# Turning listed expert rows in 32 by 32 blocks on VectorE, with rows and first weights loaded in a matching order

## The chip, the cores and the metric

The kernel runs as one program on one core of a Trainium2 chip. The metric is the device time of one execution in microseconds. Six executions were timed; the figure to compare with is their median. One further execution was recorded by the hardware profiler, and every duration below is from that one.

The core's engines are TensorE (PE; its weight loads are listed as PEld), VectorE (DVE), ScalarE (ACT), GpSimd (POOL) and SyncE (SP). In this kernel SP only issues transfers. POOL does some arithmetic and issues the transfers that go by a list of rows. All transfers run on the core's 16 DMA engines.

## The reference, cut to what matters

Inputs are float32: x is (8, 512, 256), w1 is (8, 256, 1024) and w2 is (8, 1024, 256), one slice for each of eight experts.

```
h = layernorm(x) * (1 + ca) + sa
x = x + ga * linear_attention(h)                 # 16 heads, causal, rope
h = layernorm(x) * (1 + cb) + sb                 # 4096 tokens of 256
probs = softmax(h @ router_w.T)                  # 8 experts
topv, topi = top_k(probs, 2); topv = topv / (sum(topv) + 1e-9)
for each token t and each of its two experts e:
    y[t] += topv[t, e] * (gelu(h[t] @ w1[e]) @ w2[e])
return x + gb * y
```

sa, ca, ga, sb, cb and gb come from a small product of the conditioning input. The kernel computes an expert only for the tokens that chose it, which are 8192 pairs of token and expert.

## The kernel before

**Attention and routing.** The eight sequences are worked one after another, each in four chunks of 128 tokens (the functions early, middle and late). rows_of forms each token's second-layernorm row. route picks its two experts. It gives each pair of token and expert a slot in the DRAM table slots, which has a region per expert. POOL's indirect transfers (L963, eight a sequence) scatter the rows there. A row of slots has 521 numbers: 256 of the token's normed row (D), the token's number (TID), eight weights (CW to GATE) and 256 of the gate row.

**Experts in blocks.** Filled slots are worked in blocks of 128 rows (nt = 1, a single) or 256 rows of one expert (nt = 2, a pair). The list TAKE says how many blocks are taken after each sequence; plan computes on the chip which ones, and plan_rest the rest after the last sequence. In all 40 blocks run: 13 singles and 27 pairs, and the first nine are singles. For each block:

- fetch has SP read the expert's number and load its w1 (L1216, 1 MB, as 128 partitions by 2 by 1024) and w2 (L1221, 1 MB, as 128 by 8 by 256). It reads the first slot and loads the rows into r (L1227). Tiles w1, w2 and r have three buffers each. The rows wait for the scatters of the last sequence; in plan_rest for the zeroing of the table's ends too.
- turn_rows has PE turn each 128x128 piece of the rows against an identity matrix into the PSUM tile x_ps, and ACT copies x_ps to xT (two buffers), so that the 256 numbers of a row lie along partitions. DVE forms the block's weights cw and the token list to.
- PE multiplies xT by w1 into h_ps, ACT applies gelu into g, and PE multiplies g by w2 into y_ps (one buffer). A product of 32-bit numbers is two matmul instructions, so a block has 32 of them for h_ps, and 16 for y_ps for each 128 rows.
- finish has DVE scale y_ps by cw and the gate into y, and POOL adds y to the table acc, or to the output near the end, by an indirect transfer (L1321). Before the last blocks, eight copies take acc to the output.

In partition terms w1's partition p holds rows p and 128 + p of the expert's 256 input rows (k = 0 and 1), and xT's partition p holds features p and 128 + p.

**What sets the order.** The kernel first records all work in a Plan. Each piece has an engine, a cost in us, a level and what it reads and writes. Plan.run then simulates the engines and writes out one fixed order for each. Ready work with the lowest level goes first; expert products have the high level 1000 + X.k, so attention comes before them. The engines run their lists strictly in order. All emitted operations of PE, ACT and DVE carry line L220, so they are told apart by tile. SP's transfers use eight completion semaphores in turn, and in the built order a transfer waits for the one eight places before it.

Of the kernel before, what the change touches and what calls it, by code (L numbers as in the profile page):

```python
# [11 lines left out]
I32 = mybir.dt.int32  # L12
# [7 lines left out]
HEADS = 16  # L20
HD = 16
HALF = HD // 2
PAIR = 2 * HD
GH = P // HD
LN_EPS = 1e-5
# [313 lines left out]
def kernel(  # L339
# [57 lines left out]

    SYNC = mybir.DependencyInfo(mybir.DependencyClass.Sync, mybir.DependencyReason.DATA)
    scattered = []
    gathered = []  # L400
    added = []
    copied = []
# [17 lines left out]
    def late_bank(name):  # L420
        return bank(name, "late", 4)
# [462 lines left out]
    def route(q):  # L884
        b, row = q.b, q.row

        def small(shape, tag, dtype=F32):
            return L.tile(p1, shape, tag, f"{tag}_{b}", 1, dtype)

        l3 = q.logits  # L890
        red = small([P, NC, 1], "red")
        pr = small([P, NC, E], "pr")
        dve(V.tensor_reduce, red, l3, us=0.18, axis=AX.X, op=ALU.max)
        dve(V.tensor_sub, pr, l3, red.to_broadcast([P, NC, E]))
        act(pr, pr, AF.Exp)
        dve(V.tensor_reduce, red, pr, us=0.18, axis=AX.X, op=ALU.add)
        dve(V.reciprocal, red, red)

        dve(
            V.scalar_tensor_tensor, pr, pr, LARGE, red.to_broadcast([P, NC, E]), us=0.24,  # L900
            op0=ALU.mult, op1=ALU.mult,
        )

        gt = small([P, NC, E, E], "gt")
        rank = small([P, NC, E], "rank")
        mine = pr.unsqueeze(3).to_broadcast([P, NC, E, E])
        others = pr.unsqueeze(2).to_broadcast([P, NC, E, E])
        dve(V.tensor_sub, gt, others, mine)
        dve(
            V.tensor_tensor, gt, gt, least.unsqueeze(1).to_broadcast([P, NC, E, E]), op=ALU.is_gt  # L910
        )
        dve(V.tensor_reduce, rank, gt, us=0.42, axis=AX.X, op=ALU.add)
        dve(V.scalar_tensor_tensor, pr, rank, 2.0, pr, op0=ALU.is_lt, op1=ALU.mult)

        is_in = small([P, NC, E], "is_in")
        first = small([P, NC, 2, E], "first")
        dve(V.tensor_single_scalar, is_in, rank, 2.0, op=ALU.is_lt)
        at_ps = early_bank(f"at_ps_{b}")
        with L.group("PE", 1.05):
            product(  # L920
                at_ps[:, : NC * E], earlier, is_in.rearrange("p c e -> p (c e)"),
                start=True, stop=False, skip_group_check=True,
            )
            for c in range(NC):

                product(
                    at_ps[:, (c + 1) * E : (NC + 1) * E].rearrange("p (c e) -> p c e", e=E),
                    ones, is_in[:, c, :].unsqueeze(1).to_broadcast([P, NC - c, E]),
                    start=False, stop=(c == NC - 1), skip_group_check=True,
                )  # L930
        dve(V.tensor_reduce, red, pr, us=0.18, axis=AX.X, op=ALU.add)
        dve(V.tensor_scalar_add, red, red, 1e-9 * LARGE)
        dve(V.reciprocal, red, red)
        dve(V.tensor_mul, row[:, :, CW:GATE].of("cw"), pr, red.to_broadcast([P, NC, E]))
        L.do(
            "POOL", 0.15,
            lambda: G.iota(
                row.now()[:, :, TID:CW].bitcast(I32), pattern=[[P, NC], [0, 1]], base=b * S,
                channel_multiplier=1,
            ),  # L940
            w=[row.of("tid")],
        )
        dve(
            V.tensor_tensor, first, rank.unsqueeze(2).to_broadcast([P, NC, 2, E]),
            which.unsqueeze(1).to_broadcast([P, NC, 2, E]), op=ALU.is_equal,
        )
        begin = small([P, E], "begin")
        at = small([P, NC, E], "at")
        where = small([P, NC, 2], "where")
        slot = L.tile(p2, [P, NC, 2], "slot", f"slot_{b}", 2, I32)  # L950
        dve(V.tensor_add, begin, count, first_slot)
        dve(
            V.tensor_add, at, at_ps[:, : NC * E].rearrange("p (c e) -> p c e", e=E),
            begin.unsqueeze(1).to_broadcast([P, NC, E]),
        )
        dve(V.tensor_mul, first, first, at.unsqueeze(2).to_broadcast([P, NC, 2, E]))
        dve(V.tensor_reduce, where, first, us=0.21, axis=AX.X, op=ALU.add)
        dve(V.tensor_copy, slot, where)
        dve(V.tensor_add, count, count, at_ps[:, NC * E : (NC + 1) * E])
        q.scatters = []  # L960

        def scatter(c, j):
            s = nc.gpsimd.indirect_dma_start(  # L963
                out=slots, out_offset=IndirectOffsetOnAxis(ap=slot.now()[:, c, j : j + 1], axis=0),
                in_=row.now()[:, c, :], in_offset=None,
                bounds_check=NONE - 1, oob_is_err=False,
            )
            apart(s, scattered + cleared, "a slot is of one pair of token and expert")
            apart(s, gathered, "blocks that are read are full by then")
            scattered.append(s)  # L970

        L.level += LEVEL["scatter"]
        for c in range(NC):
            for j in range(2):
                q.scatters.append(
                    L.do(
                        "POOL", 1.29, lambda c=c, j=j: scatter(c, j), r=[slot, row], landing=2.0,
                        mb=0.27,
                    )
                )  # L980
                q.scatters[-1].indirect = True


    def spans(small, n, tag):
# [221 lines left out]
    def fetch(block):  # L1206
# [1 line left out]
        L.level = TOP  # L1208
        w1_sb = L.tile(wpool, [P, KD, H], "w1", f"w1_{n}", 3)
        w2_sb = L.tile(wpool, [P, NH, D], "w2", f"w2_{n}", 3)  # L1210
        r = L.tile(pb, [P, 2, ROW], "r", f"r_{n}", 3)
        reg = {}

        def weights1():
            reg["e"] = nc.sync.value_load(block.expert_i.now(), min_val=0, max_val=E - 1)
            nc.sync.dma_start(  # L1216
                out=w1_sb.now(), in_=w1[ds(reg["e"], 1)].rearrange("o (k p) h -> p (o k) h", p=P)
            )

        def weights2():  # L1220
            nc.sync.dma_start(  # L1221
# [2 lines left out]

        def rows():
            at = nc.sync.value_load(block.slot.now(), min_val=0, max_val=NONE)
            got = nc.sync.dma_start(  # L1227
                out=r.now()[:, :nt, :],
                in_=slots[ds(at, nt * P), :].rearrange("(t p) w -> p t w", p=P),
            )  # L1230
            needed = [g for w in block.seen for g in w.given]
            behind(got, needed, "the rows of a block come before it")
            apart(got, [s for s in scattered if s not in needed], "those are of later blocks")
            gathered.append(got)

        L.do("SP", 0.6, weights1, r=[block.expert_i], w=[w1_sb], landing=2.0, mb=1.0)
        L.do("SP", 0.4, weights2, r=[block.expert_i], w=[w2_sb], landing=2.0, mb=1.0)
        L.do("SP", 0.6, rows, r=[block.slot], w=[r], after=block.seen, landing=2.0, mb=0.26 * nt)
        return block, w1_sb, w2_sb, r

    def turn_rows(fetched):

        block, w1_sb, w2_sb, r = fetched
        n, nt = block.n, block.nt
        L.level = 1000 + X.k - 1.5
        rest = block.held is not None
        x_ps = late_bank(f"x_ps_{n}") if rest else early_bank(f"x_ps_{n}")
        w = nt * P
        xT = L.tile(pb, [P, KD, 2 * P], "xT", f"xT_{n}", 2)
        with L.group("PE", 0.11 * 2 * nt, hold=[xT]):  # L1250
            for k in range(KD):
                for t in range(nt):
                    turn(x_ps[:, k * w + t * P : k * w + (t + 1) * P], r[:, t, ts(k, P)])
        L.level = TOP
        copy(xT[:, :, :w], x_ps[:, : KD * w].rearrange("p (k s) -> p k s", k=KD))
        cw = L.tile(pb, [P, 2, 1], "cw", f"cw_{n}", 3)
        cwe = L.tile(pb, [P, 2, E], "cwe", f"cwe_{n}", 3)
        dve(
            V.tensor_mul, cwe[:, :nt], r[:, :nt, CW:GATE],
            block.is_of.unsqueeze(1).to_broadcast([P, nt, E]),  # L1260
        )
        dve(V.tensor_reduce, cw[:, :nt], cwe[:, :nt], us=0.17, axis=AX.X, op=ALU.add)
        to = L.tile(pb, [P, 2], "to", f"to_{n}", 3, I32)
        dve(V.tensor_copy, to[:, :nt], r[:, :nt, TID].bitcast(I32))
        if rest:

            empty = L.tile(pb, [P, 2], "empty", f"empty_{n}", 3, I32)
# [27 lines left out]
    def finish(block, cw, to, r, y_ps):  # L1295
# [3 lines left out]
        for t in range(nt):  # L1299
            dve(  # L1300
                V.scalar_tensor_tensor, y[:, t, :].of(t), y_ps[:, ts(t, D)], cw[:, t, :],
                r[:, t, GATE:], us=0.48, op0=ALU.mult, op1=ALU.mult,
            )
        if block.at_end and X.copies is None:
            def give(b):
# [94 lines left out]
    for b in range(B):  # L1400
# [20 lines left out]
        route(q)  # L1421
        if TAKE[b][0]:
            L.level = 4 * b + 3 + LEVEL["plan"]
            blocks = plan(b, q.scatters)
            experts(blocks)
    L.level = 4 * B
    blocks, others, more_i = plan_rest(q.scatters)

    def all_of(blocks):
        experts(blocks)  # L1430
# [71 lines left out]
```

## Time and profile before

| | |
|---|---|
| median of six runs | 821.68 us (818.67 to 825.2) |
| profiled execution, whole time | 825.21 us |
| its span, first to last instruction | 823.5 us |
| mean granted TensorE clock | 0.986 |
| PE, DVE, ACT, POOL busy | 96%, 46%, 34%, 39% |
| products h_ps and y_ps on PE | 255.7 and 253.6 us busy |
| turns x_ps on PE | 134, 21.5 us busy |
| bytes moved | 154.27 MB, mean 187 GB/s |
| PE busy from 441 to 799 us | 358.0 of 358.0 us |

How to read it: busy time is the sum of the recorded instruction times on an engine; matmuls overlap, so a PE that is always busy is not PE at its peak. A group line gives the line, engine, operation, written and read tiles, shape and count, then busy us and mean ns of one, then the idle time before them and what ended it. A slice line has 40 digits, one for each fortieth of the span, in tenths busy. The DMA share is a mean over the 16 engines.

The first work on experts stands at 133.6 us and the last block's first h_ps at 799.1 us. Until 424 us blocks stand between pieces of attention and routing; from there PE does experts alone, a pair about every 14 us.

### The profile page before, as it was taken

The page shows a single profiled execution, that of the slowest core. Times are in us where ns is not written, and L with a number is a line of the kernel's source. Part 1 is how long each engine was busy: PE and PEld are TensorE (multiplying, and loading weights), DVE is VectorE, ACT ScalarE, POOL GpSimd, SP SyncE. Part 2 cuts the span into 40 slices and gives each one's busy share as a digit, 9 for nine tenths or more (in the row PEclk, how much of TensorE's full clock was granted, in tenths as well). Part 3 has the DMA queues.
Part 4 walks back from the last instruction along what each step waited for, and adds up shares of the span by engine and source line. Part 5 has one row for each costly group of instructions (what it writes and reads, how often), then busy time and mean ns, then how long its engine had stood idle before and what let it go on. Part 6 is the DMA issues. An engine that isn't in the chain of part 4 may idle for free. (4 is left out here: it accounts for less than half of the span.)

```text
span 823.5 us, 15967 instructions
## 1 busy us (share of the span) xinstructions
PE 790.7 (96%) x5998; PEld 657.0 (80%) x5998; DVE 378.0 (46%) x1290; ACT 284.1 (34%) x617; POOL 320.9 (39%) x477
## 2 busy tenths in 40 slices
PE   6899989999998999999999999999999999999995
PEld 3567657767786788789888888888988889898884
DVE  4588978788886878776363010111111111111000
ACT  2546444446564475542232122222121212222120
POOL 4734374638374464726138331312121232130133
PEclk9899998999999999999999999999999999999998
DMA  7320183965664454647579966766766878579932
GB/s 233 98 60 27 59 240 129 341 149 124 199 174 125 141 163 129 214 146 232 166 230 311 299 203 190 231 174 216 240 216 193 271 211 246 173 229 306 310 67 27
DMA packets 95167, 154.27 MB, mean 187 GB/s; under 512 B 6632, under 2 KB 69736, under 8 KB 94960
## 3 DMA queue, kind: packets, MB, share of 16 engines
q1 hardware_dynamic: 79680, 125.22, 48.7%
q0 software_dynamic: 15408, 28.00, 13.5%
q8 instruction: 49, 0.80, 0.4%
q14 instruction: 30, 0.25, 0.1%
HBM read 120.19 MB, written 37.20 MB: 191 GB/s over the span
## 5 line engine op out<-in xcount | busy, mean ns | idle before, releaser
L220 PE MATMUL h_ps<-xT,w 128*128 128x256 f32 (+1 forms) x1280 | 255.7, 349 | 2.6 <-issue 2.6
L220 PE MATMUL y_ps<-w,g 128*128 128x256 f32 x1072 | 253.6, 380 | 0.0
L220 PEld LDWEIGHTS h_ps<-xT,w 128*128 128x128 f32 x1280 | 215.1, 194 | 26.1 <-issue 3.2
L220 PEld LDWEIGHTS y_ps<-w,g 128*128 128x128 f32 x1072 | 200.2, 190 | 26.1 <-issue 0.6
L220 ACT ACTIVATE g<-h_ps 128x512 f32<-128x512 f32 x134 | 80.0, 597 | 307.3 <-PE h_ps L220 307.1
L1321 POOL DMA_INDIRECT acc<-y,to x57 | 90.3, 1584 | 243.2 <-DVE y L220 198.0
L220 DVE SCALAR_TENSOR_TENSOR y<-y_ps,cw,r 128x256 f32<-128x256 f32 x67 | 29.9, 479 | 155.1 <-PE y_ps L220 155.0
L220 DVE TENSOR_TENSOR sm<-s_ps,causal 128x512 f32<-128x512 f32 x128 | 82.1, 678 | 11.9 <-PE s_ps L220 11.9
L963 POOL DMA_INDIRECT slots<-row,slot x64 | 64.8, 1013 | 36.6 <-issue 13.2
L220 PE MATMUL qk_ps<-wqkv_sb,hT 128*128 128x512 f32 x128 | 65.0, 633 | 1.1 <-ACT hT L220 1.0
L220 POOL TENSOR_TENSOR f<-f,t 128x512 f32<-128x512 f32 x32 | 43.4, 1359 | 52.2 <-DVE t L220 41.1
L220 DVE TENSOR_TENSOR cwe<-r,is_of_rest 128x16 f32<-128x16 f32 (+1 forms) x21 | 3.6, 173 | 130.1 <-DMA r<-slots 122.3
L220 PEld LDWEIGHTS s_ps<-qT,kT 32*128 32x128 f32 x1024 | 32.6, 186 | 10.8 <-issue 7.3
L220 PE MATMUL s_ps<-qT,kT 32*128 32x128 f32 x1024 | 39.5, 284 | 0.9 <-ACT logits L220 0.7
L220 PEld LDWEIGHTS qk_ps<-wqkv_sb,hT 128*128 128x128 f32 x128 | 24.0, 202 | 20.2 <-issue 14.2
L220 PE MATMUL v_ps<-wqkv_sb,hT 128*128 128x256 f32 x128 | 36.2, 408 | 2.1 <-ACT hT L220 2.0
L220 PE MATMUL oT_ps<-sm,vz 128*32 128x128 f32 x1024 | 36.8, 276 | 1.3 <-DVE sm L220 1.2
L1321 POOL DMA_INDIRECT out_dram<-y,to x10 | 15.6, 1559 | 52.9 <-DMA out_dram<-acc 23.3
L220 POOL TENSOR_SCALAR mv_f<-mv_f 128x1 f32<-128x1 f32 x32 | 10.2, 318 | 62.5 <-DVE mv_f L220 56.2
L220 PE MATMUL a_ps<-wo,oT 128*128 128x256 f32 x128 | 33.6, 385 | 0.5 <-DVE sm L220 0.4
L220 ACT COPY xT<-x_ps 128x512 f32<-128x512 f32 (+1 forms) x40 | 20.6, 514 | 34.6 <-PE x_ps L220 34.3
L220 PEld LDWEIGHTS oT_ps<-sm,vz 128*32 128x32 f32 x1024 | 26.9, 109 | 6.7 <-DVE sm L220 3.2
(227 smaller groups left out, 998.4 us busy)
## 6 DMA issues: line engine op xcount, KB each, us to landing
w<-in_w_dram SPq DMA_DIRECT2D x80, 1024.0 KB, 5.8
r<-slots SPq DMA_DIRECT2D x27, 521.0 KB, 6.9
row<-modd SPq DMA_DIRECT2D x8, 512.0 KB, 10.1
acc<-x SPq DMA_DIRECT2D x8, 512.0 KB, 3.7
out_dram<-acc SPq DMA_DIRECT2D x8, 512.0 KB, 10.6
x<-in_x_dram SPq DMA_DIRECT2D x7, 512.0 KB, 7.1
r<-slots SPq DMA_DIRECT2D x13, 260.5 KB, 6.8
mod<-modd SPq DMA_DIRECT2D x8, 384.0 KB, 4.5
```

The costliest lines, as they stand in the source:

```text
L220: return method(now(out), *[now(a) for a in args], **{k: now(a) for k, a in kw.items()})
L963: s = nc.gpsimd.indirect_dma_start(out=slots, out_offset=IndirectOffsetOnAxis(ap=slot.now()[:, c, j : j + 1], axis=0), in_=row.now()[:, c, ...
L1321: s = nc.gpsimd.indirect_dma_start(out=out.rearrange("b s d -> (b s) d") if block.at_end else acc, out_offset=IndirectOffsetOnAxis(ap=to.n ...
```

## The change

- A block's 256 features are no longer turned by PE. The first 256 numbers of each listed row go to a new tile sx by four transfers, one for each quarter q of 64 features. Quarter q lands on the 32 partitions 32q to 32q + 31. The partition is the row's place within a group of 32 rows; along the partition lie the groups (4 nt of them), then k of 2, then 32 features. The other 265 numbers of each row go to a smaller r by a fifth transfer.
- One DVE transpose then turns every 32x32 block of sx within its own 32 partitions straight into xT. Partition 32q + c of xT holds features 64q + c and 64q + 32 + c.
- w1 is loaded to match: partition 32q + c holds input rows 64q + 32k + c for k = 0 and 1. This takes two transfers of 512 KB, one for each k, whose source is 4 by 32 by 1024.
- The bank x_ps, its turns on PE and the copy on ACT are gone. TID, CW and GATE are read from r at an offset less by D.
- The list of scatters that a block's rows wait for now holds those of all sequences so far.

In the order built for each engine, PE has the same products as before without the turns. SP issues eight transfers a block instead of three. On DVE the transpose of a block stands in the place where cwe stood, ahead of the y evictions of one or two blocks before it.

```diff
+Q = 32
...
+    scatters = []
...
-                q.scatters.append(
+                scatters.append(
...
-        r = L.tile(pb, [P, 2, ROW], "r", f"r_{n}", 3)
+        sx = L.tile(pb, [P, 8, KD, Q], "sx", f"sx_{n}", 3)
+        r = L.tile(pb, [P, 2, ROW - D], "r", f"r_{n}", 3)
...
-            nc.sync.dma_start(
-                out=w1_sb.now(), in_=w1[ds(reg["e"], 1)].rearrange("o (k p) h -> p (o k) h", p=P)
-            )
+            parts = w1[ds(reg["e"], 1)].rearrange("o (q k c) h -> k (o q) c h", k=KD, c=Q)
+            for k in range(KD):
+                nc.sync.dma_start(out=w1_sb.now()[:, k, :], in_=parts[k])
...
-            got = nc.sync.dma_start(
-                out=r.now()[:, :nt, :],
-                in_=slots[ds(at, nt * P), :].rearrange("(t p) w -> p t w", p=P),
-            )
+            rows_ = slots[ds(at, nt * P), :]
             needed = [g for w in block.seen for g in w.given]
-            behind(got, needed, "the rows of a block come before it")
-            apart(got, [s for s in scattered if s not in needed], "those are of later blocks")
-            gathered.append(got)
+            parts = [
+                (
+                    sx.now()[q * Q : (q + 1) * Q, : 4 * nt].rearrange("p t k c -> p t (k c)"),
+                    rows_[:, q * KD * Q : (q + 1) * KD * Q].rearrange("(t p) c -> p t c", p=Q),
+                )
+                for q in range(P // Q)
+            ]
+            parts.append((r.now()[:, :nt, :], rows_[:, D:].rearrange("(t p) w -> p t w", p=P)))
+            for out_, in_ in parts:
+                got = nc.sync.dma_start(out=out_, in_=in_)
+                behind(got, needed, "the rows of a block come before it")
+                apart(got, [s for s in scattered if s not in needed], "those are of later blocks")
+                gathered.append(got)
...
-        L.do("SP", 0.6, rows, r=[block.slot], w=[r], after=block.seen, landing=2.0, mb=0.26 * nt)
+        L.do("SP", 1.0, rows, r=[block.slot], w=[sx, r], after=block.seen, landing=2.0, mb=0.35 * nt)
...
-        L.level = 1000 + X.k - 1.5
+        L.level = TOP
         rest = block.held is not None
-        x_ps = late_bank(f"x_ps_{n}") if rest else early_bank(f"x_ps_{n}")
-        w = nt * P
         xT = L.tile(pb, [P, KD, 2 * P], "xT", f"xT_{n}", 2)
-        with L.group("PE", 0.11 * 2 * nt, hold=[xT]):
-            for k in range(KD):
-                for t in range(nt):
-                    turn(x_ps[:, k * w + t * P : k * w + (t + 1) * P], r[:, t, ts(k, P)])
-        L.level = TOP
-        copy(xT[:, :, :w], x_ps[:, : KD * w].rearrange("p (k s) -> p k s", k=KD))
+        dve(
+            V.transpose, xT[:, :, : nt * P].rearrange("p k (t c) -> p k t c", c=Q),
+            sx[:, : 4 * nt].rearrange("p t k c -> p k t c"),
+        )
```

## Prediction, made before the result was known

> **What bounds the kernel now.** I read the page's busy shares and slices first, then stages, then shapes, then transfers.
>
> ```profile
> PE 790.7 (96%) x5998; PEld 657.0 (80%) x5998; DVE 378.0 (46%) x1290; ACT 284.1 (34%) x617; POOL 320.9 (39%) x477
> ...
> DVE  4588978788886878776363010111111111111000
> ...
> DMA  7320183965664454647579966766766878579932
> ```
>
> PE is full and DVE nearly idle from slice 22 on. DMA is busy too, but this is a mean over 16 engines: it says nothing about a transfer that uses only some of them. By stages (columns: length, then busy us of PE, PEld, DVE, ACT, POOL; clock, DMA share, GB/s):
>
> ```profile
> 441.00:799.00 358.00, 358.00 (x1771) 316.85 (x1771) 43.10 (x188) 74.35 (x128) 90.04 (x120) 1.00 0.75 227
> ```
>
> That is 26 of the 40 blocks, PE never idle at full clock, DMA at 0.75. The removed work and its place in the stream (groups by shape: count, busy us, mean ns of one, idle before; then the order of time: start us, us):
>
> ```profile
> L220 PE MATMUL x_ps<-ident,r 128*128 128x128 f32 x134 | 21.5, 275 | 0.8 <-DVE qk L220 0.8
> ...
> L220 ACT COPY xT<-x_ps 128x512 f32<-128x512 f32 x27 | 15.8, 584 | 28.5 <-PE x_ps L220 28.5
> ```
>
> ```profile
> 604.63 1.89 PE L220 MATMUL y_ps<-w,g 128*128 128x256 f32 x8
> ...
> 606.36 0.60 PE L220 MATMUL x_ps<-ident,r 128*128 128x128 f32 x4
> ...
> 606.79 1.89 PE L220 MATMUL y_ps<-w,g 128*128 128x256 f32 x8
> ```
>
> Matmuls overlap, so 275 ns is not what a turn costs: four of them start at 606.36 and the next product starts at 606.79, so 0.43 us for four, 0.108 us each. Last the transfers (KB each, median us to landing):
>
> ```profile
> q1 hardware_dynamic: 79680, 125.22, 48.7%
> ...
> w<-in_w_dram SPq DMA_DIRECT2D x80, 1024.0 KB, 5.8
> r<-slots SPq DMA_DIRECT2D x27, 521.0 KB, 6.9
> ...
> modd<-modr SPq DMA_DIRECT2D x1, 32.0 KB
> ```
>
> **How many engines a transfer uses.** SP issues 180 transfers. The trace's packet records on its queue hold 2,872 packets of four bytes, each the completion of one engine's share. 179 x 16 + 8 is 2,872. Of the 180 only modd<-modr has an outer dimension under 16, namely 8 rows; all others have 128 or 16. So a transfer of outer dimension 8 ran on eight engines here. The new w1 halves are read by the pattern (o q) c h with q = 4: outer dimension 4 at the source, 128 partitions at the destination. No row shows the two sides differing, so the count lies between 4 (the source decides) and 16. I take 4, as the nearest row is a transfer held down by its small outer dimension. The Trainium skill ("DMA: Bandwidth & Descriptors", "Why a DMA increments its semaphore by 16 and not by 1") says the count is the largest number up to 16 that divides the slowest dimension of both patterns, and that these are the lowest-numbered engines: 4 here, the same four for both halves. It speaks against the change, and by it the sum is that for four engines.
>
> **The change part by part.** *Removed:* 134 turns x 0.108 = 14.4 us of PE, all on its path while PE is the bound, and 20.6 us of xT copies on ACT, which waits 307.1 us for h_ps anyway: worth nothing. *Added on DVE:* 27 block turns of 512 elements a partition and 13 of 256. No row shows this operation; bounds are the 128x2 copy at 173 ns and the 128x512 f op at 757 ns. I take the masking row of the same size, 678 ns: 27 x 0.68 + 13 x 0.4 = 24 us, in a stage where DVE is busy 43 of 358 us. Hidden; without cover at most 0.4 us a block over today's copy. *Added on SP:* five more issues a block. An issue takes 0.37 us, w2 to rows 1.2 us today, so 2 to 6 us a block of 14, not the bound. The wider scatter list adds waits on scatters that are long over: nothing.
>
> *Transfers.* From packet records, the ns of one packet, median (mean): 4096 B 159 (190), 1024 B 46 (57), 2084 B 86 (99), 64 B 11, POOL's 1024 B additions 102 (108). Engines 0 to 3, as I call the four, get of a pair block:
> - w1: 2 x 32 packets of 4096 B, 64 x 0.159 = 10.2 us (today 16 packets, 2.5 us)
> - w2: 64 of 1024 B, 64 x 0.046 = 2.9 us
> - sx: 64 of 256 B. Bounds 11 and 46 ns; on the line between them 18, so 1.1 us
> - r: 16 of 1060 B, 0.75 us
> - additions: 16 x 0.102 = 1.6 us
> - completions, about 0.1 us
>
> Sum 16.7 us for a pair. A single has the same w1 and w2, half of the rest: 14.9. Isolated w1 transfers took 3.25 us from first to last packet where 2.54 is pure, so some loss at the head is real: I take 17.0 and 15.3. On PE a pair takes 14.2 us now (h 558.5 to 572.6 to 586.8) and 13.8 without turns, a single 7. So four of the 16 engines become the bound, while the other twelve stand idle half the time. The page's own mean (0.487 x 16 x 823.5 us / 125.22 MB = 51.2 engine-us per MB) would make w1 13.4 us; it is the far end.
>
> The Trainium skill (same page, "Specifications") puts the smallest transfer at line rate at 512 B. As an estimate from it, a 256 B packet at the price of a 512 B one would be about 27 ns, 0.6 us more a pair, some 13 us in all; the 64 B row at 11 ns does not point to it.
>
> **When the four engines fill.** Three weight buffers let w1 of block n be issued when h of n-3 ends. Blocks 0 to 8 are singles, with h starts 12 to 63 us apart against 15.3 of transfer and weights issued 28 us or more ahead of need: no stall. From block 10 (w1 issued at 376.3) the queue is chained: 376 to 393, 410, 427, 443. So from block 14, at 443, engines 0 to 3 never rest again. PE lives on its lead (about 10 us) until block 20 or so. Blocks 14 to 39 are 22 pairs and 4 singles: 22 x 17.0 + 4 x 15.3 = 435 us. The eight out<-acc copies (16 packets of 32 KB each, 1.5 us an engine) add 12, landing 2.
>
> In the built order the DVE turn of a block stands ahead of the y evictions of one or two blocks before. DVE waits there for sx, and behind it are y, POOL's addition, and PE, since y_ps has one buffer. So PE runs about a block behind the rows: no loss while transfers bind, but some 10 us at the end. Last h start to end of span is 24 us now (799.1 to 823.5). Sum: 443 + 435 + 12 + 2 + 10 + 24 = 926 us of span, 928 with the 1.7 us around it (825.21 beside 823.5). The profiled execution stands 0.4% above the median 821.68, so the forecast against the median is about 924; I say 922.
>
> **The rivals.**
> 1. *All 16 engines carry w1* (the destination's 128 decides). Then a block needs 16.7 - 7.6 = 9 us of each engine against 13.8 of PE, PE stays the bound, and the 14.4 us come off: 825.2 - 14.4 = 811, about 807 against the median. For it: the destination still has 128 partitions. Against it: the eight-row transfer. It decides where w1 takes under 7.4 us of an engine (13.8 less the other 6.4), that is on six engines or more.
> 2. *Sixteen engines, but rows land late.* Five issues and small packets add 3 to 8 us to landing. Against it: rows land 11 us or more ahead of h (block 23: landed 580.1, h at 592.1). Beyond that slack each us costs up to 40 us; 4 us past it in the 26 late blocks, 104 us less the turns' 14, gives about 911; one us, about 834.
> 3. *Four engines, but hidden.* A packet would have to take 115 ns; the shortest 4096 B packet of the trace took 156. It would give about 820.
>
> **How the numbers follow.** Four engines that bind 0.83, rival 1 0.12, rival 2 0.03, rival 3 0.02. Low end: shortest packets (156, 44, 9 ns) make 15.7 and 14.3 a block, 403 for 435, no lag at the end, and the copies hidden in gaps: 870. High end: packet means and sx at 23 ns make 20 and 17.7, 511 for 435: 1000. Outside lie rivals 1 and 3 and a few hundredths above. Faster by over 0.5% (about what a measurement here can tell from no change) is rival 1, 0.12; same 0.02; slower 0.86.
>
> **What would show it.** Right: four-byte packets of q1 fall short of 16 per transfer by 12 for each of 80 w1 halves; w landing near 8 to 15 us; mean DMA share falls below 0.75 in the late stage while PE waits for w there; block starts 17 us apart after pairs, about 15 after singles. x_ps and the xT copies are gone; a DVE transpose of 128x512 stands near 0.7 us. Wrong: landing of w stays near 5 us and block starts are 13.8 us apart. Also wrong in size, if stalls already begin in the attention part, or if waits end on sx rather than on weights.

## The result, and the profile after

The changed kernel took 1038.27 us (median of 20 runs, 1027.01 to 1048.7). The kernel before took, in 46 runs with it, 822.75 us (818.19 to 827.48). The ratio is 1.2594, 95% interval 1.2565 to 1.2623; it leaves disturbed runs out and so differs a little from that of the medians. The forecast was 922 us with a range of 870 to 1000. The direction was right. The size was not: the loss is 216 us where 100 were forecast.

The profiled execution of after has a span of 1033.2 us. First its page: busy shares, the clock and DMA slices, SP's queue, and three groups (busy us, mean ns of one, idle before and what ended it).

```profile
PE 821.6 (80%) x5864; PEld 672.0 (65%) x5864; DVE 401.6 (39%) x1330; ACT 274.9 (27%) x585; POOL 316.6 (31%) x477
...
PEclk9999989689899999998998989999898887897978
DMA  6502735555555654367877567566575666667741
...
q1 hardware_dynamic: 116224, 125.23, 46.4%
...
L221 PE MATMUL y_ps<-w,g 128*128 128x256 f32 x1072 | 277.2, 406 | 124.5 <-issue 119.4
...
L221 DVE STREAM_TRANSPOSE xT<-sx 128x512 f32<-128x512 f32 (+1 forms) x40 | 25.0, 624 | 382.5 <-DMA sx<-slots 346.5
...
w<-in_w_dram SPq DMA_DIRECT2D x80, 512.0 KB
```

PE falls from 96% to 80% busy, and the same bytes as before are moved. The turns cost DVE about what was estimated: 25.0 us in all against 24. But DVE stands 346.5 us waiting for rows. Then the stage that was full before (columns: length, then busy us of PE, PEld, DVE, ACT, POOL; clock, DMA share, GB/s):

```profile
441.00:799.00 358.00, 281.72 (x1330) 241.13 (x1328) 60.04 (x252) 49.63 (x87) 79.68 (x114) 0.91 0.67 165
```

PE was busy in all 358 us; now in 282. The mean DMA share falls from 0.75 to 0.67 although the transfers have become the bound: this mean covers 16 engines, and w1 now uses four of them (the count is given below). Who waits from h of block 14 (526 us) to h of block 39 (1009 us; engine, tile and what it waited for: us in all, times, longest):

```profile
DVE xT L221 <- DMA sx<-slots: 312.6, 22, 17.5
```

PE's own idle time stands under "issue", which names no releaser (119.4 us before y_ps). How DVE's wait reaches PE is seen in the order of time (start us, us, idle before in brackets):

```profile
656.42 0.71 DVE L221 STREAM_TRANSPOSE xT<-sx 128x512 f32<-128x512 f32 x1 [16.40 <-DMA sx<-slots]
...
657.85 0.87 DVE L221 SCALAR_TENSOR_TENSOR y<-y_ps,cw,r 128x256 f32<-128x256 f32 x2
...
658.82 3.65 PE L221 MATMUL y_ps<-w,g 128*128 128x256 f32 x8 [4.64 <-issue]
```

DVE waits 16.40 us for sx, turns, and only then empties y_ps; PE's next product into y_ps starts 0.1 us after that.

Last, SP's own list in one round of that stage (start us, us, transfers, how many):

```profile
652.83 1.54 SPq L1224 DMA_DIRECT2D w<-in_w_dram  x2
655.05 0.40 SPq L1227 DMA_DIRECT2D w<-in_w_dram  x1
656.78 11.74 SPq L1244 DMA_DIRECT2D sx<-slots  x4
668.77 0.36 SPq L1244 DMA_DIRECT2D r<-slots  x1
669.99 1.42 SPq L1224 DMA_DIRECT2D w<-in_w_dram  x2
```

The four row transfers take 11.74 us to issue. One of the four, the second, takes 10.2; most issues take 0.3 to 0.9. An issue that takes several times as long is called held below. From one pair of w1 issues to the next it is 17.2 us here (a single); over blocks 15 to 37 the mean is 18.84 for a pair and 17.2 for a single, where 17.0 and 15.3 were forecast. The page gives no time to landing for w or sx, so that sign of the forecast can't be read.

### The profile page after: what moved, and what is told of

The parts are those of the page before. It is cut to its first block, busy times and chain, and to the rows that moved or that the text cites. A ratio compares the mean times of both kernels' runs of the same rounds, so it can differ in the third digit from the quotient of the medians.

```text
span 1033.2 us, 16373 instructions
## 1 busy us (share of the span) xinstructions
PE 821.6 (80%) x5864; PEld 672.0 (65%) x5864; DVE 401.6 (39%) x1330; ACT 274.9 (27%) x585; POOL 316.6 (31%) x477
## 5 line engine op out<-in xcount | busy, mean ns | idle before, releaser
L221 PE MATMUL y_ps<-w,g 128*128 128x256 f32 x1072 | 277.2, 406 | 124.5 <-issue 119.4
L221 PEld LDWEIGHTS y_ps<-w,g 128*128 128x128 f32 x1072 | 214.7, 204 | 162.2 <-issue 124.8
L221 PE MATMUL h_ps<-xT,w 128*128 128x256 f32 (+1 forms) x1280 | 271.7, 362 | 36.9 <-issue 33.5
L221 PEld LDWEIGHTS h_ps<-xT,w 128*128 128x128 f32 x1280 | 226.9, 204 | 66.2 <-issue 39.2
L221 DVE STREAM_TRANSPOSE xT<-sx 128x512 f32<-128x512 f32 (+1 forms) x40 | 25.0, 624 | 382.5 <-DMA sx<-slots 346.5
L221 PE MATMUL oT_ps<-sm,vz 128*32 128x128 f32 x1024 | 39.3, 284 | 3.0 <-DVE sm L221 2.9
L221 PEld LDWEIGHTS v_ps<-wqkv_sb,hT 128*128 128x128 f32 x128 | 23.2, 199 | 6.8 <-ACT hT L221 3.0
```

What stands on the lines that cost most here:

```text
L221: return method(now(out), *[now(a) for a in args], **{k: now(a) for k, a in kw.items()})
```

## The experiments

They ran on other chips than the first runs: e1 to e4 on one, where the kernel before took 870.79 us, e5 to e8 on a second and e9 on a third, on each of which it took 869.73 us. Each ratio is to the kernel before on the same chip. Times that were expected for e1 to e4 start from the 822 us of the first chip, so compare by ratio. Block times are starts of h_ps from the profiles. "Late" is from h of block 14 to h of block 39.

**e1: w1 in four transfers instead of two.** The new layout of w1 is kept; each transfer has a slowest dimension of 32.

```diff
-            parts = w1[ds(reg["e"], 1)].rearrange("o (q k c) h -> k (o q) c h", k=KD, c=Q)
-            for k in range(KD):
-                nc.sync.dma_start(out=w1_sb.now()[:, k, :], in_=parts[k])
+            parts = w1[ds(reg["e"], 1)].rearrange("o (q k c) h -> q (o c) k h", k=KD, c=Q)
+            for q in range(P // Q):
+                nc.sync.dma_start(out=w1_sb.now()[q * Q : (q + 1) * Q], in_=parts[q])
```

> The changed kernel, with w1 in four transfers of 32 partitions by 2 by 1024 (source 32 by 2 by 1024) in place of two halves whose source is 4 by 32 by 1024. Bytes, rows, the DVE turns and their order stay. Theory A (a w1 half runs on four engines, because its source pattern's outer dimension is 4, and these four bind): all 380 + 80 transfers post 16 completions (7,352 four-byte packets on SP's queue, 8 short of 16 each only for modd), w1 lands in about 5 us, a pair takes 13.8 us again, 805 to 815 us. Rival B (the five row transfers with 256-byte runs, their issue on SP, or the DVE turn that waits ahead of the y evictions makes the time): nothing of that is changed, and SP issues two more transfers a block, so 1000 us or more.

Measured: 868.4 us, ratio 0.997 (0.9938 to 1.0002). Late takes 325.8 us. The window from h of block 14 to that of block 39:

```profile
514.30:840.10 325.80, 320.28 (x1538) 282.99 (x1536) 53.36 (x203) 54.93 (x92) 73.19 (x92) 0.99 0.93 223
```

SP's queue now holds 7,352 four-byte packets: each of the 460 transfers but modd<-modr posts 16, as theory A had it. PE is nearly full again, so the loss of after lies in how w1 is loaded. But the gain that theory A expected is missing: w1's 4096-byte packets take 309 ns in the median of this stage, against 159 in before, and the DMA share is 0.93. Each of these transfers writes to only 32 partitions. The Trainium skill ("SBUF — State Buffer", "Door 1: The DMA port swizzle") says that 32 neighbouring partitions reach 8 of the 16 ports that DMA writes through. A packet of twice the length agrees with that.

**e2: the kernel before with only w1's two halves.** PE still turns the rows; w1's rows land where the new order puts them, so the expert products meet the wrong rows of w1.

```diff
-            nc.sync.dma_start(
-                out=w1_sb.now(), in_=w1[ds(reg["e"], 1)].rearrange("o (k p) h -> p (o k) h", p=P)
-            )
+            parts = w1[ds(reg["e"], 1)].rearrange("o (q k c) h -> k (o q) c h", k=KD, c=32)
+            for k in range(KD):
+                nc.sync.dma_start(out=w1_sb.now()[:, k, :], in_=parts[k])
```

> The kernel before, with only the w1 load of the change: two halves with the source 4 by 32 by 1024. PE turns the rows as before. The features of a row then meet the wrong rows of w1, so the expert's products differ from the reference; nothing else is left out. Theory A: four engines get per pair 12.8 of w1, 4.4 of w2, 1.5 of rows, 1.9 of additions, so the late stage has a block about every 18 us and the time is 990 to 1040 us. Rival B (rows and DVE turn): under 840 us. For the loss in the attention part: if it comes from eight transfers a block against eight completion semaphores, the first product of block 14 stands near 480 us here, since a block has four; if from the four engines' queue, near 515 to 525 us, as in the changed kernel.

Measured: 1051.37 us, ratio 1.2092 (1.1994 to 1.2191), late 463.1 us. This one edit brings nearly the whole loss, without the DVE turn and without the five row transfers. It has four transfers a block where after has eight, so the number of transfers isn't the cause either. Block 14 starts at 559.6 us. On a chip about as slow (e5), before reaches it 39 us later than on the first chip; less these it is 520, the place expected for the four engines' queue and not the 480 for the semaphores.

**e3: only one of the two halves on few engines.** The half for k = 0 stays as in after; k = 1 goes in four transfers of 32 partitions.

```diff
-            for k in range(KD):
-                nc.sync.dma_start(out=w1_sb.now()[:, k, :], in_=parts[k])
+            nc.sync.dma_start(out=w1_sb.now()[:, 0, :], in_=parts[0])
+            for q in range(P // Q):
+                nc.sync.dma_start(out=w1_sb.now()[q * Q : (q + 1) * Q, 1, :], in_=parts[1][q])
```

> The changed kernel with half the dose: w1's half k = 0 by the transfer of source 4 by 32 by 1024, half k = 1 by four transfers of 32 by 1024. The four engines then get 32 + 8 packets of w1 a block, 6.4 us at 159 ns in place of 10.2, and 12.8 us in all against 13.8 of PE for a pair. Theory A with its threshold (w1 under 7.4 us of an engine is hidden): 810 to 840 us, w1's first half landing at 7 to 8 us. A cost that follows the dose with no threshold: half of the loss, about 925 us.

Measured: 966.54 us, ratio 1.1088 (1.0999 to 1.1177), late 407.6 us. The expectation missed: the half that is left on four engines isn't hidden. w1's packets don't keep their old price; those of both halves together take 245 ns in the mean of the late stage. The second half's transfers write to 32 partitions at a time, as in e1, and run beside the first. Half the dose costs near half the loss (late is 79 us over that of before, after's 154).

**e4: w2 loaded once.** The other 39 loads of w2 are left out, so all later blocks use the first block's w2.

```diff
+            self.w2 = None
...
-        w2_sb = L.tile(wpool, [P, NH, D], "w2", f"w2_{n}", 3)
+        once = X.w2 is None
+        if once:
+            X.w2 = L.tile(wpool, [P, NH, D], "w2", f"w2_{n}", 3)
+        w2_sb = X.w2
...
-        L.do("SP", 0.4, weights2, r=[block.expert_i], w=[w2_sb], landing=2.0, mb=1.0)
+        if once:
+            L.do("SP", 0.4, weights2, r=[block.expert_i], w=[w2_sb], landing=2.0, mb=1.0)
```

> The changed kernel, with w2 loaded once, for the first block, and that tile used by all blocks: 39 of 40 w2 loads are left out, and the products with w2 are those of one expert. It asks why a 4096-byte packet took 201 ns on average in the late stage and not 159 to 165. Theory C (w1's packets on the four engines are slowed while w2 runs on the other twelve): no such packets are left, the mean falls to 165 to 180 ns, the four engines need 14 us a pair and 13 a single, and the time is 830 to 880 us. Theory D (packets of a four-engine transfer are slow by themselves, as they all write through few ports): the mean stays near 200, a pair needs 16.5 us, and the time is 910 to 950 us.

Measured: 954.8 us, ratio 1.0974 (1.0909 to 1.1039). Late is 368.8 us, with PE busy in 331.80 of them and a DMA share of 0.50:

```profile
567.10:935.90 368.80, 331.80 (x1538) 287.41 (x1537) 51.75 (x203) 54.95 (x92) 73.27 (x92) 0.96 0.50 131
```

The packets came as expected: 164 ns median, 180 mean in that stage. The whole did not: block 14 starts at 567.1 us, no earlier than in e2 (559.6). So leaving out w2 helps the late stage alone, and there may be a second loss ahead of block 14, which these runs can't tell from a difference between chips. The next runs separate the two. (Leaving out w2 also takes its own time off the four engines, so the whole doesn't give the price of the slowed packets; the packet times do.)

**e5 and e6: before and after, unchanged, one profile each on one chip.**

> The unchanged kernel of before, profiled beside the others on one chip, because the chip of the earlier runs ran it in 871 us and the first chip in 822 us. Theory A (chips differ where attention runs): blocks 14 to 39, from h start to h start, take 328 us here as they did before (within 3 us), and a difference of the whole, if this chip shows one, lies ahead of block 14, where attention end moves past 424 us. Rival: a slower chip is slower everywhere; then blocks 14 to 39 stretch in proportion (348 us for 871).

> The unchanged kernel of after, profiled on the same chip. Set beside the unchanged kernel of before on this chip it gives the two shares of the loss free of the difference between chips. Theory: the late stage keeps its 18.45 us a block (14 to 39 about 483 us), whatever the chip, and the attention part ends 55 to 60 us later than that of before on the same chip. Rival: the late attention end was the chip's, then it ends within 10 us of before here and the loss ahead of block 14 is only what the weights cost.

Measured: 864.57 and 1070.34 us, one time each. The late windows of e5 and e6:

```profile
510.20:838.50 328.30, 328.30 (x1629) 290.71 (x1628) 40.55 (x178) 68.09 (x117) 73.44 (x92) 1.00 0.73 221
```

```profile
562.10:1044.10 482.00, 354.25 (x1537) 302.34 (x1537) 51.99 (x205) 54.94 (x92) 73.23 (x92) 0.87 0.64 156
```

Both take what they took on the first chip (328.3 and 482.7). What the chips differ in lies ahead of block 14: the same kernel reaches it at 510.2 us here and at 470.8 there. Its cause was not looked into. On this chip after reaches block 14 at 562.1 us. The loss is thus 52 us ahead of block 14 and 154 us behind it.

**e7: halves for the first 14 blocks, quarters after.**

```diff
+            self.count = 0
...
+        late = X.count >= 14
+        X.count += 1
...
+            if late:
+                parts = w1[ds(reg["e"], 1)].rearrange("o (q k c) h -> q (o c) k h", k=KD, c=Q)
+                for q in range(P // Q):
+                    nc.sync.dma_start(out=w1_sb.now()[q * Q : (q + 1) * Q], in_=parts[q])
+                return
```

> The first 14 blocks load w1 as after does (two transfers on four engines), the later 26 blocks in four transfers of 32 partitions by 2 by 1024, which run on 16 engines. Theory S (the slip of the start comes from the early blocks' own w1 halves, which fill four engines while attention runs): attention ends as late as in after (some 55 us past before on this chip), and then blocks 14 to 39 take about 326 us as with quarters, so the whole is before's time plus 35 to 55 us, ratio about 1.04 to 1.07. Rival R (the start slips because the late chain is ahead in SP's queue, or because of the DVE turns and the five row transfers): then the attention end stays late also with quarters everywhere, and this kernel's time equals that of quarters everywhere, ratio about 1.00. Rival Z (the early blocks' halves cost nothing, the first singles being far apart): attention ends within 10 us of before, ratio 1.00 or below.

Measured: 916.65 us, ratio 1.0509 (1.045 to 1.0567). Block 14 starts at 562.8 us, as in e6, and late then takes 329.0 us:

```profile
562.80:891.80 329.00, 321.37 (x1538) 283.34 (x1537) 53.54 (x203) 54.93 (x92) 73.24 (x92) 0.99 0.95 222
```

So the early loss comes from the first 14 blocks' own halves, and the late loss from the later ones. The two add up. How much of the early 52 us is due to the halves is seen beside e8.

**e8: w1 in neighbouring pairs of rows, one transfer.** DVE's turn stays. Partition p of w1 holds rows 2p and 2p + 1, which is one piece of 8 KB in DRAM; the turn reads every second number of a row instead.

```diff
-        sx = L.tile(pb, [P, 8, KD, Q], "sx", f"sx_{n}", 3)
+        sx = L.tile(pb, [P, 8, Q, KD], "sx", f"sx_{n}", 3)
...
-            parts = w1[ds(reg["e"], 1)].rearrange("o (q k c) h -> k (o q) c h", k=KD, c=Q)
-            for k in range(KD):
-                nc.sync.dma_start(out=w1_sb.now()[:, k, :], in_=parts[k])
+            nc.sync.dma_start(
+                out=w1_sb.now(), in_=w1[ds(reg["e"], 1)].rearrange("o (p k) h -> p (o k) h", p=P)
+            )
...
-            sx[:, : 4 * nt].rearrange("p t k c -> p k t c"),
+            sx[:, : 4 * nt].rearrange("p t c k -> p k t c"),
```

> The block turn of DVE is kept, but w1 is loaded by one transfer whose partition p holds the two neighbouring input rows 2p and 2p + 1 (8 KB in one piece of DRAM, outer dimension 128, so 16 engines and all 128 partitions at once). The rows in sx then lie as 32 columns by 2, and the DVE turn reads every second number. Theory (the loss is all in how w1 is loaded): PE is the bound again without the turns, blocks 14 to 39 take 315 to 326 us against 328, and the whole is 5 to 14 us below before, ratio 0.983 to 0.994. w1 packets cost about 160 ns per 4096 bytes again, not the 283 of quarters into 32 partitions. Rival (the five row transfers a block or the DVE turn cost as much as the PE turns gave): ratio 1.00 or above, with PE waiting for sx or xT in the late stage. The stride of two in the DVE turn may cost up to 0.7 us more a block on DVE, hidden beside PE.

Measured: 860.19 us, ratio 0.9873 (0.9823 to 0.9923), a little faster than the kernel before. The late window, and two groups of its page:

```profile
517.00:835.20 318.20, 318.20 (x1537) 281.83 (x1537) 53.36 (x203) 54.94 (x92) 72.65 (x92) 1.00 0.80 228
```

```profile
L221 PE MATMUL y_ps<-w,g 128*128 128x256 f32 x1072 | 255.2, 381 | 4.3 <-ACT g L221 2.0
...
L221 DVE STREAM_TRANSPOSE xT<-sx 128x512 f32<-128x512 f32 (+1 forms) x40 | 24.9, 623 | 135.1 <-PE h_ps L221 91.5
```

PE never rests at full clock, a pair takes 13.8 us, and late is 10.1 us shorter than in e5. That is the price of the turns in it: 21 pairs of 0.43 us and four singles of 0.22 make 9.9. The stride costs DVE nothing (712 ns in the median for a turn of 128x512, 711 without). An 8192-byte packet of w1 takes 309 ns in the median, about the old rate per byte.

Ahead of block 14 e8 doesn't gain: it starts that block at 517.0 us, 6.8 later than e5. With one profile of each, how much of this is chance isn't shown. It does split the 52 us: e6 and e7 start block 14 at 562.1 and 562.8, so the early halves account for some 45 us, and the other 7 are there without them.

**e9: SP's list changed in one place.** In after's built order SP issues the weights of blocks 2 and 3 (counting from 0) before the rows of block 1. Here they stand behind these rows (X.given holds each block's w1, w2 and rows).

```diff
...
+        if X.given[1][2] in L.order:
+            back = [w for g in X.given[2:4] for w in g[:2]]
+            at = L.order.index(X.given[1][2])
...
+            back.sort(key=L.order.index)
+            L.order[at + 1 : at + 1] = back
+            for w in back:
+                L.order.remove(w)
```

> After, with only SP's list changed in one place: the weights of the third and fourth block (four halves and two w2) stand behind the rows of the second block instead of ahead of them. In after two of these halves are held about 10 us each in their issue, with the store of the sequence held 10.8 behind them, and the second block's rows are issued at 203 us where one transfer on 16 engines for w1 had them at 181; its h starts at 213 against 193. Theory H (the start slips because SP, held in issuing to the full four engines, issues the next rows late): rows of the second block are issued by about 185 and its h starts 15 to 20 us earlier than in after on this chip, and some of that stays to the end, 5 to 20 us of the whole (ratio to before 1.21 to 1.225, after on this chip 1.231). Rival F (the rows would be late anyway, being queued behind weights on the four engines, or for want of scatters): h of the second block stays within 5 us of 213 and the whole at 1065 to 1075 us. A later start for the third and fourth block, whose weights now come after, could give all of it back; then the h of block 3 stands near 279 as in after.

What it changes is seen against SP's list in after, from the first profile:

```profile
153.83 13.23 SPq L1224 DMA_DIRECT2D w<-in_w_dram  x2
167.27 1.26 SPq L1227 DMA_DIRECT2D w<-in_w_dram  x1
169.60 13.21 SPq L1224 DMA_DIRECT2D w<-in_w_dram  x2
183.06 1.83 SPq L1227 DMA_DIRECT2D w<-in_w_dram  x1
185.00 10.61 SPq L1423 DMA_DIRECT2D acc<-x  x1
195.93 1.51 SPq L855 DMA_DIRECT2D row<-modd  x1
198.49 2.79 SPq L1244 DMA_DIRECT2D sx<-slots  x4
```

Three issues hold SP for 10 us and more, one behind the other, and the rows of block 1 are issued only at 198.5 us, though all packets of its w1 had ended by 168. PE waits 21.7 us for h of block 1. In e9:

```profile
179.88 0.37 SPq L1426 DMA_DIRECT2D acc<-x  x1
180.60 0.36 SPq L855 DMA_DIRECT2D row<-modd  x1
182.60 4.39 SPq L1245 DMA_DIRECT2D sx<-slots  x4
187.19 0.36 SPq L1245 DMA_DIRECT2D r<-slots  x1
188.35 1.40 SPq L1225 DMA_DIRECT2D w<-in_w_dram  x2
190.35 0.40 SPq L1228 DMA_DIRECT2D w<-in_w_dram  x1
191.83 10.97 SPq L1225 DMA_DIRECT2D w<-in_w_dram  x2
203.04 1.85 SPq L1228 DMA_DIRECT2D w<-in_w_dram  x1
205.88 11.63 SPq L1245 DMA_DIRECT2D sx<-slots  x4
```

Rows of block 1 are issued at 182.6 and its h starts at 194.9 us, as theory H had it (213.0 in e6, where h of block 0 starts 0.7 us from that of e9). But the held issues only move: now the rows of block 2 stand behind them, its h starts at 255.3 us against 247.7, and block 14 at 571.3 against 562.1. The whole is 1084.6 us, ratio 1.2436 (1.2322 to 1.255), against 1.231 for e6's one execution: no gain. What was expected of the start held; what was expected of the whole didn't.

## Why the prediction was wrong in size

**Right: w1's halves run on four engines.** SP issues 380 transfers. The trace has 5,112 four-byte packets on its queue: 380 x 16, less 8 for modd<-modr, less 80 x 12 for the halves, exactly as forecast. In the late stage at most six w1 packets overlap, and mostly four, where before has about 15. So of 4 at the source and 128 at the destination the 4 decides. The Trainium skill ("DMA: Bandwidth & Descriptors", "Why a DMA increments its semaphore by 16 and not by 1") says the same. Rival 1 (16 engines) is out, and e8 shows about what it would have brought: 1.3% off. Rival 2 is out as the main cause: e1 and e8 keep the five row transfers.

**Right: the DVE turn, the small packets, the end.** A turn takes 711 ns for 128x512 against 678 estimated. A 256-byte packet takes 18 ns in the median, as read off the line between 64 and 1024 bytes. From the last rows landed (997.9) to the end it is 35 us, where 34 were put down (a lag of 10, a tail of 24).

**The sign named for "wrong in size" appeared.** Waits end on sx rather than on weights, since the rows go last into the same queue; and stalls begin in the attention part.

The forecast span was 926 us and the measured one 1033.2. The 107 us between them:

| step of the prediction | forecast | measured | error |
|---|---|---|---|
| w1 of block 14 issued at | 443 | 495.2 | +52.2 |
| block 14, w1 issue to next w1 issue | 17.0 | 25.6 | +8.6 |
| blocks 15 to 37 (19 pairs, 4 singles) | 384.2 | 426.5 | +42.3 |
| block 38 to the last rows landed | 48 | 50.6 | +2.6 |
| rows to end | 34 | 35.3 | +1.3 |

Less the 52.2 us of the first row the measured median would be 986 us, less the 42.3 of the third 996, either inside the stated range. So both failed steps were needed to leave it.

**Failed step 1: "Blocks 0 to 8 are singles ... no stall", and the chain from block 10 that starts from it.** That compared the transfer time of a block with the time between blocks. It left out that SP's list is one queue, and it priced an issue at 0.37 us, the median of before, where the longest already took 4.5. A held issue stops everything behind it: the rows of earlier blocks and the store of a sequence. Weights were early enough, as forecast: for blocks 1 to 13 the last w1 packet ended 24 us or more ahead of h. Rows were not: those of block 1 wait in the list behind weights that nobody needs yet. Block 10's w1 is issued at 396.2 us where 376.3 was put down, and 32 us more are lost by block 14.

e7 shows that the early halves cause this loss; e9 shows that the held issues do it at block 1, and that moving one place isn't enough. Beside e8, h of e6 is 20 us late at block 1, 37 at block 9 and 45 at block 14. The first 20 are the held issues. How the other 25 arise isn't shown. A slower TensorE may have a part in it: in the 60 us from 190 us on, PE of e6 stands still longer than that of e8 and has a lower granted clock, 0.74 against 0.97 (e6, then e8; columns as above):

```profile
190.00:250.00 60.00, 36.80 (x309) 29.00 (x310) 26.54 (x102) 15.54 (x34) 21.03 (x31) 0.74 0.56 164
```

```profile
190.00:250.00 60.00, 55.60 (x548) 43.10 (x547) 43.92 (x155) 29.18 (x62) 27.95 (x40) 0.97 0.56 169
```

A held issue of sx ends when w1 is nearly through. By the packet records of after, each of the 24 that take over 8 us from 525 us on begins with 190 to 224 of the 256 packets of the w1 ahead of it not yet started and ends with 14 to 44 left. Which limit this is (packets, bytes or transfers) stays open.

**Failed step 2: "64 x 0.159 = 10.2 us."** The term was mis-sized: w1's packets took 201 ns in the mean of the late stage, so 12.8 us. The median of before was taken, from a state in which about 15 w1 packets are under way at once. In after about four are, and many w2 packets run beside them; the records name no engine, and that these are on the other twelve is inferred from the counts: where nine or more run, it is mostly 12 to 14, beside four of w1. By the number of w2 packets under way in the middle of a w1 packet (packet records; before from 441 to 799 us, after in the late stage):

| w2 packets under way | before, mean (median) ns | after, mean (median) ns | share of after's |
|---|---|---|---|
| none | 187 (159) | 176 (165) | 58% |
| 1 to 8 | 163 (159) | 196 (165) | 14% |
| 9 and more | 162 (159) | 254 (269) | 28% |

The last line of before rests on 1% of its packets. But e4 takes w2 away and the packets are at 180 (164) again: the slow ones go with w2. Of a pair's 18.84 us w1 is 12.8 (2.6 over). For w2 3.4 is an estimate (0.5 over; 64 packets at 53 ns, the mean of those with fewer than four w1 packets under way). What is left, 2.6, is 1.3 under the forecast; why isn't shown, and it hides part of the error of w1 by luck. Had the mean of before been taken, 190, w1 would have been 12.2. Why a w1 packet is slowed by packets on other engines is not shown; that they share a way to or from a memory is only a guess.

## What to carry to other kernels

Look at the outer dimension of both sides of a transfer before looking at its bytes: here a layout that left 4 there put the transfer on four engines, and the mean DMA share even fell. When a transfer changes the engines it runs on, price its packets by the mean, and ask what will run beside it; and when a queue can be held at issue, look in its list at what stands behind, since that, not the transfer itself, may be what comes late. Another order of the same data may keep both sides wide: pairs of neighbouring rows did here, with a stride on an engine that had time.

## What the runs showed of the hardware

- An issue on SP, usually 0.3 to 0.9 us, can be held for long where transfers on few engines are queued: 8.5 to 12.4 us in after, up to 11.7 in e2, and many of 3 to 7 in e3 and e4. In e8 no issue took over 2.1 us, in before none over 4.5.
- In transfers on 16 engines a 4096-byte packet took 309 ns in the median where each transfer writes to 32 partitions (e1), and 159 ns where it writes to 128 (before).
- In after a 4096-byte packet of a transfer on four engines took 165 ns in the median with no w2 packet under way, and 269 ns with nine or more. In before, with w1 on 16 engines, it was 159 ns in each case.
- A DVE transpose of 32x32 blocks in 32 bits took 711 ns in the median for 128x512 and 445 ns for 128x256; with a stride of two in its source 712 and 445 (e8).
